# Five score bursts for two head groups in place of six, and mixing two bursts behind, in the attention stage of a hybrid block

## The chip, the cores and the metric

The kernel runs on one core of a Trainium2 chip. The metric is the device time of one execution in microseconds (us); the number given for the kernel before is the median of 8 runs. The engines are named as the profile does: PE is TensorE's matrix multiplication and PEld its weight load, DVE is VectorE, ACT is ScalarE, POOL is GpSimd, SP is SyncE, whose queue issues most of the DMAs.

## What is computed

The input x has 8 batches of 512 rows of 256 numbers, all in fp32. The block is a chain of two mixers, each followed by the same kind of expert layer, each with layer norm ahead and a residual sum behind. The first mixer is a state scan. The second is causal attention with 16 heads of 16 numbers each, and it is the one that matters here:

```
def attn(x, Wqkv, Wout):
    qkv = einsum('btd,ed->bte', x, Wqkv).reshape(b, t, 3, H, DK).transpose(2, 0, 3, 1, 4)
    q, k, v = qkv[0], qkv[1], qkv[2]
    scores = clip(einsum('bhtd,bhsd->bhts', q, k) / sqrt(DK), -10.0, 10.0)
    attn = softmax(scores + triu(full((t, t), -1e9), k=1), axis=-1)
    out = einsum('bhts,bhsd->bhtd', attn, v).transpose(0, 2, 1, 3).reshape(b, t, d)
    return einsum('btd,ed->bte', out, Wout)
```

The expert layer has 16 experts of which each row takes 4 (chosen within 2 of 4 groups), and two shared experts that every row passes through.

## The kernel before

**Stages.** The program has four stages one after another: the scan stretch, the routed experts of the first expert layer, the attention stretch, and the routed experts of the second. `stretch(layer)` writes a mixer batch by batch, and puts beside it, so that TensorE has work: the projections of the next batch (`project`), the shared experts of the batch two before (`shared_experts`), the route of the batch before (`Route`: layer norm, logits, choice of the experts, places, sending of the rows by indirect DMA), and the load, layer norm and turning of the batch two ahead. Loading a batch in the attention stretch means two DMAs (`load_sum`, L152 to L165): the tile `more` and the tile `x`, which VectorE then adds in two halves (L163). The load of `x` stands in SP's queue behind the store of the batch before and behind the store of its normed rows. Only batches 2 to 7 are loaded so, during batches 0 to 5; batches 0 and 1 were readied in the stage before.

**What sets the order.** A mixer is a generator that yields after each portion of matmuls the number of columns that it has streamed. `beside()` (L346) always takes the next portion of the piece that has done the smallest share of its columns; `timed()` (L362) puts the steps of a chain of small operations at given shares of the whole: the two halves of the load's sum at 0.24 and 0.28, the layer norm of the batch ahead from 0.32 to 0.44 and from 0.56 to 0.64, the route's steps at 0.0 to 0.95. A scheduler then sets the instructions on the engines; where they wait follows from the tiles that they share. Each engine works its own queue in order.

**PSUM.** In the attention stretch the pool `one` has four banks, which the projections `pq` (queries and keys) and `pv` (values), the accumulators `po`, the route's `pl` and `pr`, the shared experts' `pg` and `pd` and the output projection `py` take in turn, and the pool `pair` has two tiles of two banks for scores. A bank comes free when its last reader is done: for `pr` that is the addition of `where_m` (L713), for a key projection it is the copy L1196 on VectorE, which makes the second of two key tiles.

**Attention.** The 16 heads of a batch are two halves `o` of 8 heads; a half has two groups `w` of 4 heads (`HG`). The 4 heads of a group lie in four row groups of 32 partitions and are worked by TensorE side by side. Scores are made transposed: for a chunk `c` of 128 keys, all queries from the chunk's first on are columns, so that chunk 0 has 512, chunk 1 has 384, chunk 2 has 256 and chunk 3 has 128. `weights()` (L1223) makes one burst: the scores (L1240) of the chunks named in `BANKS[i]` into two `pair` tiles (two heads each), the exponential of each tile on ScalarE (L1251), and the clamps on VectorE: L1254 for the square on the diagonal, which also masks, and L1262 for the rest. `BANKS` gives a group three bursts: chunk 0 (512 columns), chunks 3 and 1 (128 and 384), chunk 2 (256). The results of full bursts lie in one of 6 "es" spots of the idle expert weights `w_all` (`spot`, L1151), those of the 256-column burst in a work tile `es_a` of the tag "col".

`mix()` (L1267) multiplies the values with the results of a burst (L1275) and sums them up in `po`, a bank for each group; the values have a column of ones, so that the sum of the weights comes along. `share()` (L1285) turns `po` round (L1288), divides, and after the second group turns the half back for the output projection. `steps()` (L1300) puts them in order: with each burst of a group goes the mixing of the burst of the same number of the group before, so mixing lags by three bursts, and a group's mixing ends while the next but one has not begun. In batches 2 to 6 (`close`) scores and mixing are yielded as one portion; in 0, 1 and 7 other work may come between them.

Of the kernel before, what the change touches and what calls it, by code (L numbers as in the profile page):

```python
# [10 lines left out]
FP = mybir.dt.float32  # L11
AF = mybir.ActivationFunctionType
ALU = mybir.AluOpType
AX = mybir.AxisListType

P = 128
SQ = 32
QUAD = P // SQ
B, T, D = 8, 512, 256
# [7 lines left out]
NO = H * DK // P  # L27
# [32 lines left out]
KB, COLS = 9, 6  # L60
# [10 lines left out]
ATT_SCALE = 0.25  # L71

TOP, LOW = float(np.exp(CLIP)), float(np.exp(-CLIP))

BANKS = [((0,), 4 * P), ((3, 1), 4 * P), ((2,), 2 * P)]


@with_exitstack  # L80
def tile_hybrid_block(
# [22 lines left out]
    nc = tc.nc  # L104
# [3 lines left out]
    work = ctx.enter_context(tc.tile_pool(name="work", bufs=2))  # L108
# [4 lines left out]
    def bank(shape, name: str, kind: str = "one"):  # L113
        kind = instead.get(kind, kind)
        return stage[kind].tile(shape, FP, tag=kind, name=name)
# [153 lines left out]
    causal = const.tile([P, 2, P], FP, name="causal")  # L269
# [27 lines left out]
    groups = const.tile([P, P // E], FP, name="groups")  # L297
# [177 lines left out]
    def add_projection(b: int, lhs_of, w_sb, n: int, tag: str):  # L475

        x_sb = x_tiles[b]
        for half in range(2):
            py = bank([P, 2, D], f"py_{tag}_{half}")
            for j in range(2):  # L480
                t = 2 * half + j
                for c in range(n):
                    nc.tensor.matmul(  # L483
                        py[:, j, :],
                        lhsT=lhs_of(c)[:, t * P : (t + 1) * P],
                        rhs=w_sb[:, c, :],
                        start=(c == 0),
                        stop=(c == n - 1),
                    )
                yield n * D  # L490
            rows = x_sb[:, 2 * half : 2 * half + 2, :]
            nc.vector.tensor_add(rows, py, rows)
# [658 lines left out]
    def spot(kind: str, rows: int):  # L1151
        first, many, n = spots[kind]
        spots[kind][2] = (n + 1) % many
        at = first_expert * WEXP + (first + n) * NT * D
        return w_all[:, at : at + NT * D].rearrange("p (a b) -> p a b", a=rows)

    class Attention:
# [60 lines left out]
        def main(self, b: int, made):  # L1218
            q_sb, k_sb, v_sb = made
            tag = f"a{b}"  # L1220
            held = {}

            def weights(o: int, w: int, i: int, at):  # L1223


                tiles, cols = BANKS[i]
                ps, es = [], []
                for two in range(2):
                    name = f"{tag}_{o}_{w}_{i}_{two}"
                    ps.append(bank([P, 2, T], f"ps_{name}", "pair"))  # L1230
                    if cols == T:
                        es.append(spot("es", 2))
                    else:
                        es.append(work.tile([P, 2, cols], FP, tag="col", name=f"es_{name}", bufs=COLS))
                col = 0
                for c in tiles:
                    n = T - c * P
                    for j in range(HG):
                        r = slice(32 * j, 32 * j + 32)
                        nc.tensor.matmul(  # L1240
                            ps[j // 2][:, j % 2, col : col + n],
                            lhsT=k_sb[w][r, o, c * P : (c + 1) * P],
                            rhs=q_sb[r, o, c * P : T],
                            start=True,
                            stop=True,
                        )
                        at[c, j] = es[j // 2][:, j % 2, col : col + n]
                    col += n
                mixed = len(tiles) * P
                for two in range(2):  # L1250
                    nc.scalar.activation(es[two], ps[two][:, :, 0:cols], AF.Exp, scale=ATT_SCALE)  # L1251
                    diagonal = es[two][:, :, 0:mixed]
                    limit = causal[:, 0 : len(tiles), :].rearrange("p c q -> p (c q)")
                    nc.vector.scalar_tensor_tensor(  # L1254
                        diagonal,
                        diagonal,
                        LOW,
                        limit.unsqueeze(1).to_broadcast([P, 2, mixed]),
                        ALU.max,
                        ALU.min,  # L1260
                    )
                    nc.vector.tensor_scalar(es[two][:, :, mixed:], es[two][:, :, mixed:], LOW, TOP, ALU.max, ALU.min)  # L1262
                return T + (len(tiles) - 1) * T

            order = [c for tiles, _ in BANKS for c in tiles]

            def mix(o: int, w: int, i: int, at):  # L1267


                if i == 0:  # L1270
                    at["po"] = bank([P, T], f"po_{tag}_{o}_{w}")
                for c in BANKS[i][0]:
                    for j in range(HG):
                        h = 8 * o + 2 * j + w
                        nc.tensor.matmul(  # L1275
                            at["po"][32 * j : 32 * j + 32, c * P : T],
                            lhsT=v_sb[:, c, h * VC : h * VC + 32],
                            rhs=at[c, j],
                            start=(c == order[0]),
                            stop=(c == order[-1]),  # L1280
                            tile_position=(0, 32 * j),
                        )
                return len(BANKS[i][0]) * T

            def share(o: int, w: int, at):  # L1285

                tr = work.tile([P, T // SQ, SQ], FP, tag="col", name=f"tr_{tag}_{o}_{w}", bufs=COLS)
                nc.vector.transpose(tr.rearrange("p q c -> p (q c)"), at["po"])  # L1288
                rec = small.tile([P, T // SQ], FP, tag="rec", name=f"rec_{tag}_{o}_{w}")
                nc.vector.reciprocal(rec, tr[:, :, DK])  # L1290
                both = held.setdefault(o, tr)
                nc.vector.tensor_mul(
                    both[:, :, w * DK : (w + 1) * DK],
                    tr[:, :, 0:DK],
                    rec.unsqueeze(2).to_broadcast([P, T // SQ, DK]),
                )
                if w == 1:
                    nc.vector.transpose(held["oT"][:, o, :], both.rearrange("p q c -> p (q c)"))

            def steps():  # L1300
                held["oT"] = work.tile([P, NO, T], FP, tag="kb4", name=f"oT_{tag}", bufs=KB)
                groups = [(o, w, {}) for o in range(NO) for w in range(2)]

                close = 1 < b < B - 1
                last = None
                for o, w, at in groups:
                    for i in range(len(BANKS)):


                        columns = weights(o, w, i, at)  # L1310
                        if last is not None and not close:
                            yield columns
                            columns = 0
                        if last is not None:
                            columns += mix(*last[0:2], i, last[2])
                        yield columns
                    if last is not None:
                        share(*last)
                        yield 0
                    last = o, w, at  # L1320
                for i in range(len(BANKS)):
                    yield mix(*last[0:2], i, last[2])
                share(*last)
                yield 0
                yield from add_projection(b, lambda c: held["oT"][:, c, :], wo_sb, KD, tag)

            return Piece(2 * NO * 2 * NT * T + NT * KD * D, steps())


# [48 lines left out]
    def stretch(layer):  # L1378
# [40 lines left out]
        def first_two():  # L1419

            layer.load(1)
            issue(Piece(0, norm(1, True)))
            for _ in range(2):
                pending.pop(0)()
            main = layer.main(0, made.pop(0))
            issue(Piece(0, some(main.steps, NI)))
            issue(Piece(0, turn(1)))
            issue(project(1))
            second = layer.main(1, made.pop(1))
            issue(Piece(0, some(second.steps, NI)))  # L1430
            issue(main)
            return Piece(second.columns - NI * KD * T, second.steps)
# [185 lines left out]
```

## Time and profile before

| what | us |
|---|---|
| median of 8 runs (lowest, highest) | 1718.51 (1715.83, 1723.56) |
| profiled execution: time | 1715.33 |
| profiled execution: span | 1713.6 |
| PE busy in the span | 1603.8 (94%) |
| DVE busy | 1149.7 (67%) |
| ACT busy | 750.2 (44%) |
| attention stage, from the first score to the last output projection | 772.8 to about 1242 |
| scores L1240 in it | 121.7 |
| mixing L1275, full bursts and 256-column ones | 73.3 and 21.1 |

The mean granted clock of TensorE is 0.977 over the span and 1.00 from 765 to 1184 us. The first scores of the batches start at 772.82, about 818, 867, 931.75, 995.37, 1058.77, 1122.91 and 1185.57 us: the middle batches take 63 to 64 us each. The page gives busy times by engine and, for the costliest groups of instructions, line, engine, operation, tiles (out<-in), busy time and the mean in ns, and after the bar the idle time of the engine just before them with what ended it. In a timeline the columns are start, length, engine, line, operation and tiles, how many instructions are gathered in the row, and in brackets the idle time before. TensorE's matmuls overlap, so the cost of one group is best read from its start to the start of the next.

### The profile page before, as it was taken

The numbers are of one execution on the slowest core, as the hardware profiler recorded it, in microseconds if no ns is written. First come the engines' busy times: TensorE is split into PE (matmuls) and PEld (weight loads), VectorE is DVE, ScalarE is ACT, GpSimd is POOL, SyncE is SP. The second block draws the span as 40 slices with busy tenths as digits, with TensorE's granted clock in tenths as the row PEclk, the third lists the DMA queues.
The fourth block names the chain that finished last, engine by engine and source line by source line (L and its number), as shares of the span: only waits on it lengthen the run. The fifth ranks groups of instructions, "written<-read, shape, count | busy, mean of one in ns | idle before, by whom it ended". The sixth has DMA issues, their size and how long they took to land.

```text
span 1713.6 us, 34252 instructions
## 1 busy us (share of the span) xinstructions
PE 1603.8 (94%) x9996; PEld 1162.4 (68%) x9996; DVE 1149.7 (67%) x3685; ACT 750.2 (44%) x1494; POOL 758.8 (44%) x655
## 2 busy tenths in 40 slices
PE   6899995969999999999999999999996999999996
PEld 3566663649999999983344444444355999999995
DVE  7977875525667766646887977967752566666664
ACT  3222322115555555546544444443312555555553
POOL 3355554525555555550022422422451555555554
PEclk8999998989999999999999999999998999999998
DMA  4354422436777766641233323232542767777776
GB/s 162 125 182 167 136 85 81 166 88 98 105 116 122 106 98 97 100 62 37 75 97 120 97 85 120 85 94 76 163 166 68 106 92 129 133 133 135 133 134 132
DMA packets 278815, 192.95 MB, mean 113 GB/s; under 512 B 167041, under 2 KB 260001, under 8 KB 278625
## 3 DMA queue, kind: packets, MB, share of 16 engines
q1 hardware_dynamic: 225536, 117.04, 27.0%
q0 software_dynamic: 51984, 72.09, 23.7%
q8 instruction: 85, 1.39, 0.3%
q10 hardware_dynamic: 1104, 1.57, 0.3%
q14 instruction: 106, 0.86, 0.2%
HBM read 87.36 MB, written 103.23 MB: 111 GB/s over the span
## 4 chain that ended last, share of the span: by engine, by line
PE 35%; DVE 8%; DMA 5%; issue 2%; SPq 2%; ACT 1%; another core or an unknown queue 0%; POOL 0%; POOLq 0%; DVEq 0%; ACTq 0%
PE ph L990 11%; PE pyr L1021 5%; PE ps_a L1240 4%; DMA part<-rows 4%; PE pg_m L1102 3%; PE po_a L1275 3%; PE pd_m L1131 3%; PE pq_a L1185 2%; PE pv_a L1203 1%; PE py_a L483 1%; SPq L944 1%; DVE w_all L1254 1%; DVE act_m L1118 1%; DVE w_all L1262 1%; DVE sig_m L1117 1%
## 5 line engine op out<-in xcount | busy, mean ns | idle before, releaser
L1031 POOL DMA_INDIRECT part<-rows x272 | 426.5, 1568 | 345.9 <-ACT rows L1030 223.4
L756 POOL DMA_INDIRECT xg<-sorted_m,slots_m x256 | 257.7, 1007 | 329.2 <-ACT slots_m L753 75.3
L990 PEld LDWEIGHTS ph<-rows,gate 128*128 128x128 f32 x2160 | 279.0, 192 | 29.7 <-ACT rows L973 17.6
L990 PE MATMUL ph<-rows,gate 128*128 128x128 f32 x2160 | 291.7, 278 | 0.0
L990 PE MATMUL ph<-rows,up 128*128 128x128 f32 x2160 | 285.6, 275 | 0.0
L1021 PE MATMUL pyr<-w_all,rows 128*128 x1088 | 278.9, 380 | 0.0
L990 PEld LDWEIGHTS ph<-rows,up 128*128 128x128 f32 x2160 | 263.3, 192 | 0.0
L963 DVE COPY up<-w_all 128x512 f32 x270 | 119.2, 442 | 213.7 <-PE ph L990 183.6
L963 ACT COPY gate<-w_all 128x512 f32 x270 | 166.3, 618 | 118.9 <-DVE up L963 51.5
L1021 PEld LDWEIGHTS pyr<-w_all,rows 128*128 128x128 f32 x1088 | 187.0, 192 | 14.4
L1030 ACT ACTIVATE rows<-pyr,gain 128x256 f32<-128x256 f32 x272 | 128.7, 473 | 80.6 <-PE pyr L1021 55.3
L998 ACT ACTIVATE rows<-ph 128x256 f32<-128x256 f32 x272 | 104.3, 383 | 120.1 <-PE ph L990 99.6
L1251 ACT ACTIVATE w_all<-ps_a 128x1024 f32<-128x1024 f32 x128 | 124.5, 1020 | 55.7 <-PE ps_a L1240 46.0
L1000 DVE TENSOR_TENSOR rows<-ph,rows 128x256 f32<-128x256 f32 x272 | 115.2, 423 | 43.5 <-ACT rows L998 30.4
L1240 PE MATMUL ps_a<-w_all 32*128 32x384 f32 (+3 forms) x1024 | 121.7, 470 | 11.9 <-ACT w_all L1251 10.2
L1001 DVE TENSOR_TENSOR rows<-ph,rows 128x256 f32<-128x256 f32 x272 | 115.2, 424 | 25.7 <-PE ph L990 0.8
L1102 PE MATMUL pg_m<-xT_m,su_sb 128*128 128x512 f32 x256 | 124.7, 609 | 0.0
L1131 PE MATMUL pd_m<-sd_sb,act_m 128*128 128x256 f32 x512 | 122.2, 383 | 1.7 <-DVE act_m L1118 1.5
L1102 PE MATMUL pg_m<-xT_m,sg_sb 128*128 128x512 f32 x256 | 122.3, 600 | 0.0
L1131 PEld LDWEIGHTS pd_m<-sd_sb,act_m 128*128 128x128 f32 x512 | 95.4, 190 | 26.9 <-issue 7.0
L1240 PEld LDWEIGHTS ps_a<-w_all 32*128 32x128 f32 x1024 | 48.2, 184 | 77.9 <-ACT w_all L1251 30.3
L1102 PEld LDWEIGHTS pg_m<-xT_m,sg_sb 128*128 128x128 f32 x256 | 47.1, 192 | 58.3 <-issue 51.1
(218 smaller groups left out, 2062.2 us busy)
## 6 DMA issues: line engine op xcount, KB each, us to landing
rows<-xg SPq DMA_DIRECT2D x712, 32.0 KB
rows<-xg SPq DMA_DIRECT2D x94, 134.0 KB
part<-x SPq DMA_DIRECT2D x16, 512.0 KB
part<-ys_m SPq DMA_DIRECT2D x14, 512.0 KB
sum<-part SPq DMA_DIRECT2D x14, 512.0 KB
w_all<-in_L_ffn_gate_w_dram SPq DMA_DIRECT2D x24, 256.0 KB
w_all<-in_L_ffn_up_w_dram SPq DMA_DIRECT2D x24, 256.0 KB
w_all<-in_L_ffn_down_w_dram SPq DMA_DIRECT2D x24, 256.0 KB
```

The source lines that it names most:

```text
L756: nc.gpsimd.indirect_dma_start(out=xg[i], out_offset=bass.IndirectOffsetOnAxis(ap=slots[:, at : at + 1], axis=0), in_=rows[:, t, :], in_of ...
L963: copy(here, w_all[:, bass.ds(held[n][0] + half * KD * F, KD * F)])
L990: nc.tensor.matmul(ph[s][:, f * P : (f + 1) * P], lhsT=both[s][:, k * F + f * P : k * F + (f + 1) * P], rhs=rows[:, ROW + k * P : ROW + (k ...
L1000: nc.vector.tensor_mul(act, ph[0], act)
L1001: made = nc.vector.tensor_mul(act, ph[1], act)
L1021: nc.tensor.matmul(py, lhsT=act[:, f * P : (f + 1) * P], rhs=w_all[:, bass.ds(w + 2 * KD * F + f * D, D)], start=(f == 0), stop=(f == KF - 1),
L1030: nc.scalar.mul(y, py, gain[:, TK : TK + 1])
L1031: acc = nc.gpsimd.indirect_dma_start(out=parts[i][n % 2], out_offset=bass.IndirectOffsetOnAxis(ap=rows[:, D + 2 * TK : D + 2 * TK + 1].bit ...
L1102: made = nc.tensor.matmul(dst, lhsT=w[:, k, f * P : (f + 1) * P], rhs=xnT[:, k, :], start=(k == 0), stop=(k == KD - 1),)
L1131: nc.tensor.matmul(py[:, j, :], lhsT=acts[n][:, f, t * P : (t + 1) * P], rhs=shared[n][3][:, f, :], start=(n == 0 and f == 0), stop=(n == ...
L1240: nc.tensor.matmul(ps[j // 2][:, j % 2, col : col + n], lhsT=k_sb[w][r, o, c * P : (c + 1) * P], rhs=q_sb[r, o, c * P : T], start=True, st ...
L1251: nc.scalar.activation(es[two], ps[two][:, :, 0:cols], AF.Exp, scale=ATT_SCALE)
```

## The change

`BANKS` now gives the five bursts of a half, each entry a pair of group and chunk. Both groups' chunks 2, of 256 columns each, share one burst, with their group-0 columns first. All results lie in the "es" spots, so no `es_a` tiles are left. The exponential of every burst covers 1024 columns; for the shared burst the clamps take the two diagonal squares and the two rests together. Mixing lags by `LAG` = 2 bursts, whatever the group; the accumulators of both groups of a half are open at the same time. The rest of `main`, and every other stage, has the same text.

```
-BANKS = [((0,), 4 * P), ((3, 1), 4 * P), ((2,), 2 * P)]
+BANKS = [((0, 0),), ((0, 3), (0, 1)), ((1, 0),), ((0, 2), (1, 2)), ((1, 3), (1, 1))]
+LAG = 2
...
-            def weights(o: int, w: int, i: int, at):
...
+            def weights(o: int, i: int, at):
+
+
+                ps = [bank([P, 2, T], f"ps_{tag}_{o}_{i}_{two}", "pair") for two in range(2)]
+                es = [spot("es", 2) for _ in range(2)]
                 col = 0
-                for c in tiles:
+                for w, c in BANKS[i]:
...
+                    nc.scalar.activation(es[two], ps[two], AF.Exp, scale=ATT_SCALE)
+                    if len({w for w, _ in BANKS[i]}) > 1:
+                        each = es[two].rearrange("p j (w q) -> p (j w) q", w=2)
+                        diagonal, full = each[:, :, 0:P], each[:, :, P:]
+                        limit = causal[:, 0, :].unsqueeze(1).to_broadcast([P, 4, P])
+                    else:
...
+                    nc.vector.scalar_tensor_tensor(diagonal, diagonal, LOW, limit, ALU.max, ALU.min)
+                    nc.vector.tensor_scalar(full, full, LOW, TOP, ALU.max, ALU.min)
...
+            def mix(o: int, i: int, at):
+
+
+                ended = []
+                for w, c in BANKS[i]:
+                    places = [c for which, c in order if which == w]
+                    if c == places[0]:
+                        at["po", w] = bank([P, T], f"po_{tag}_{o}_{w}")
...
+                    if c == places[-1]:
+                        ended.append(w)
+                return len(BANKS[i]) * T, ended
...
-                groups = [(o, w, {}) for o in range(NO) for w in range(2)]
+                made = [{} for _ in range(NO)]
+                bursts = [(o, i, made[o]) for o in range(NO) for i in range(len(BANKS))]
...
-                last = None
-                for o, w, at in groups:
-                    for i in range(len(BANKS)):
...
+                for n in range(len(bursts) + LAG):
+                    columns, ended = 0, []
+                    if n < len(bursts):
+                        columns = weights(*bursts[n])
+                        if n >= LAG and not close:
                             yield columns
                             columns = 0
...
+                    if n >= LAG:
+                        o, i, at = bursts[n - LAG]
+                        more, ended = mix(o, i, at)
+                        columns += more
+                    yield columns
+                    for w in ended:
+                        share(o, w, at)
                         yield 0
```

In the changed kernel's text the lines up to L1223 stand one lower (L164 is L163 of before, L714 is L713, L1197 is L1196, L1204 is L1203); scores are L1234, the exponential L1244, the clamps L1254 and L1255, mixing L1270, and `po` is turned round at L1285.

More of the change, by code (lines that the diff above doesn't have):

```diff
@@ L1221, in main @@
             held = {}
-            def weights(o: int, w: int, i: int, at):
[L1226 to L1234, printed above, removed]
+            def weights(o: int, i: int, at):
+                ps = [bank([P, 2, T], f"ps_{tag}_{o}_{i}_{two}", "pair") for two in range(2)]
+                es = [spot("es", 2) for _ in range(2)]
                 col = 0
-                for c in tiles:
+                for w, c in BANKS[i]:
                     n = T - c * P
@@ L1246, in weights @@
                         )
-                        at[c, j] = es[j // 2][:, j % 2, col : col + n]
+                        at[w, c, j] = es[j // 2][:, j % 2, col : col + n]
                     col += n
-                mixed = len(tiles) * P
                 for two in range(2):
[L1251 to L1272, printed above, removed]
+                    nc.scalar.activation(es[two], ps[two], AF.Exp, scale=ATT_SCALE)
[4 more added lines that the diff above has]
+                    else:
+                        mixed = len(BANKS[i]) * P
+                        diagonal, full = es[two][:, :, 0:mixed], es[two][:, :, mixed:]
+                        limit = causal[:, 0 : len(BANKS[i]), :].rearrange("p c q -> p (c q)")
+                        limit = limit.unsqueeze(1).to_broadcast([P, 2, mixed])
@@ new lines, in weights @@
+                    nc.vector.scalar_tensor_tensor(diagonal, diagonal, LOW, limit, ALU.max, ALU.min)
+                    nc.vector.tensor_scalar(full, full, LOW, TOP, ALU.max, ALU.min)
+                return len(BANKS[i]) * T
+            order = [key for keys in BANKS for key in keys]
+            def mix(o: int, i: int, at):
[4 more added lines that the diff above has]
+                        at["po", w] = bank([P, T], f"po_{tag}_{o}_{w}")
@@ L1275, in mix @@
                         nc.tensor.matmul(
-                            at["po"][32 * j : 32 * j + 32, c * P : T],
+                            at["po", w][32 * j : 32 * j + 32, c * P : T],
                             lhsT=v_sb[:, c, h * VC : h * VC + 32],
-                            rhs=at[c, j],
-                            start=(c == order[0]),
-                            stop=(c == order[-1]),
+                            rhs=at[w, c, j],
+                            start=(c == places[0]),
+                            stop=(c == places[-1]),
                             tile_position=(0, 32 * j),
                         )
-                return len(BANKS[i][0]) * T
+                    if c == places[-1]:
+                        ended.append(w)
+                return len(BANKS[i]) * T, ended
             def share(o: int, w: int, at):
                 tr = work.tile([P, T // SQ, SQ], FP, tag="col", name=f"tr_{tag}_{o}_{w}", bufs=COLS)
-                nc.vector.transpose(tr.rearrange("p q c -> p (q c)"), at["po"])
+                nc.vector.transpose(tr.rearrange("p q c -> p (q c)"), at["po", w])
                 rec = small.tile([P, T // SQ], FP, tag="rec", name=f"rec_{tag}_{o}_{w}")
@@ L1301, in steps @@
                 held["oT"] = work.tile([P, NO, T], FP, tag="kb4", name=f"oT_{tag}", bufs=KB)
-                groups = [(o, w, {}) for o in range(NO) for w in range(2)]
+                made = [{} for _ in range(NO)]
+                bursts = [(o, i, made[o]) for o in range(NO) for i in range(len(BANKS))]
                 close = 1 < b < B - 1
-                last = None
-                for o, w, at in groups:
-                    for i in range(len(BANKS)):
-                        columns = weights(o, w, i, at)
-                        if last is not None and not close:
+                for n in range(len(bursts) + LAG):
[3 more added lines that the diff above has]
+                        if n >= LAG and not close:
                             yield columns
                             columns = 0
[L1314 to L1318, printed above, removed]
-                        yield 0
[L1320 to L1324, printed above, removed]
+                    if n >= LAG:
[5 more added lines that the diff above has]
+                        share(o, w, at)
+                        yield 0
                 yield from add_projection(b, lambda c: held["oT"][:, c, :], wo_sb, KD, tag)
```

## The prediction

> **What bounds the kernel now.** I read the page first, then the table of busy times by stretch, the waits of TensorE inside the attention stage, its timeline in one batch, and the chain of waits. On the page:
>
> ```profile
> PE 1603.8 (94%) x9996; PEld 1162.4 (68%) x9996; DVE 1149.7 (67%) x3685; ACT 750.2 (44%) x1494; POOL 758.8 (44%) x655
> ...
> L1251 ACT ACTIVATE w_all<-ps_a 128x1024 f32<-128x1024 f32 x128 | 124.5, 1020 | 55.7 <-PE ps_a L1240 46.0
> L1240 PE MATMUL ps_a<-w_all 32*128 32x384 f32 (+3 forms) x1024 | 121.7, 470 | 11.9 <-ACT w_all L1251 10.2
> ```
>
> TensorE is the wall; ScalarE mostly waits for scores, and TensorE waits only 10.2 us in all for its exponentials. Where? The table by stretch, one row about a batch (length, then busy time of PE, PEld, DVE, ACT, POOL, and the granted clock):
>
> ```profile
> 800.00:870.00 70.00, 63.70 (x472) 28.58 (x472) 58.03 (x170) 33.23 (x46) 4.53 (x5) 1.00 0.29 79
> ...
> 996.50:1060.00 63.50, 63.08 (x391) 29.29 (x390) 50.50 (x157) 28.14 (x48) 20.14 (x20) 1.00 0.34 102
> ...
> 1184.00:1250.00 66.00, 58.39 (x371) 26.97 (x370) 52.48 (x175) 24.76 (x44) 25.58 (x28) 0.97 0.45 146
> ```
>
> The reader is to see two kinds of batch: in the middle ones (2 to 6) TensorE is busy for 99% and VectorE for 80%; in 0, 1 and 7 TensorE is idle for 6 to 8 us. From 933 to 1124 us TensorE's whole waiting is:
>
> ```profile
> PE pd_m L1131 <- DVE act_m L1118: 1.0, 3, 0.3
> PE pv_a L1203 <- DVE where_m L713: 0.2, 1, 0.2
> ```
>
> The second, 0.2 us long, is the tip of a second chain, as long as TensorE's own work. The chain of waits goes through it in batch 5:
>
> ```profile
> 1064.67 5.62 DMA x<-part
> ...
> 1070.48 0.69 DVE x L163
> ...
> 1075.15 0.14 DVE where_m L713
> ...
> 1075.34 1.13 PE pv_a L1203 x4
> ```
>
> A row load lands, VectorE (held until then at L163, its queue in order) works off what is queued behind, and the last of that frees the bank that the value projection needs. In batches 3, 4, 5 VectorE waited 4.03, 3.81, 4.56 us there. This chain, not its busy share, makes VectorE dangerous.
>
> **What goes.** Only the attention stage (770 to 1242 us) changes; in the others the two programs have the same order. Timeline of TensorE in batch 4:
>
> ```profile
> 1008.45 1.07 PE L1275 MATMUL po_a<-w_all,v_a 128*32 128x128 f32 x16
> ...
> 1012.25 0.70 PE L1240 MATMUL ps_a<-w_all 32*128 32x256 f32 x4
> 1012.88 1.13 PE L1203 MATMUL pv_a<-w_att,xT_l 128*128 128x256 f32 x4
> 1013.94 0.70 PE L1240 MATMUL ps_a<-w_all 32*128 32x256 f32 x4
> ...
> 1028.00 0.71 PE L1240 MATMUL ps_a<-w_all 32*128 32x256 f32 x8
> ...
> 1035.69 1.15 PE L1240 MATMUL ps_a<-w_all 32*128 32x128 f32 x16
> ```
>
> From start to start, a score burst of 512 columns takes 1.07 us (8 matmul passes), one of 128 and 384 takes 1.08 (16 passes), one of 256 takes 0.64: half the columns cost 60%. So about 0.2 us of a burst is fixed, and it is not per matmul. Two bursts of 256 make 1.28; joined, 1.08 by the 16-pass row. Per half 1.07+1.08+0.64 twice is 5.58, after it is 1.07+1.08+1.07+1.08+1.08 = 5.38: 0.4 per batch. More lies in the splits. The burst of 256 at 1012.25 was cut in two by the value projection and cost 0.63 twice, 0.63 lost, and two others started 0.17 and 0.47 later than their columns explain (they follow an exponential closely). I add up the twelve score bursts of batch 4, by starts, to 13.53 us. In the changed program's order there are ten, one still cut (+1.05, as at 1016.20 before) and the first follow-up still late (0.17): 10.76+1.22 = 11.98. **Saved on scores 1.55.** Mixing bursts go 1.00, 1.00, 0.57: 10.39 by starts in batch 4, after it ten of 1.00: **saved 0.39.** Together 1.94 per middle batch.
>
> The Trainium skill, "TensorEngine Tiling (Array Packing)", section Instruction Overhead, says that each matmul carries about 60 cycles. The change keeps the number of score matmuls, so by that rule the burst merging saves nothing, and dropping 1.94 in eight batches would put my sum at about 15 us slower. The equal 1.07 and 1.08 of 8 and 16 passes speak for a cost per burst, so I go by the rows.
>
> ScalarE: 8 x 1.02 + 4 x 0.60 = 10.56 per half become 10 x 1.02 = 10.2. VectorE: the clamps of a half lose 1.1/2 us. Both run beside TensorE, which is busy for 63.1 of 63.5 us: nothing counted. If that cover were gone, as in batches 0, 1 and 7, at most 0.36 and 0.55 us per half would count, and they lie within the bounds taken there. No DMA is added or taken away; in SP's queue one store changes places with one load in batch 1, and I cost it at nothing (the load at L163 there was 1.96 us late, which bounds it).
>
> **What comes.** Mixing now follows its scores by two bursts instead of three, and both accumulators of a half overlap, so one bank of the four single ones is held longer. The mix of two bursts ago is ready after exp 1.02 and clamps 0.60+0.34; between lie a whole burst and its exponentials (2 x 1.02), so it waits only where VectorE's queue is late.
>
> There it is late, in the batches that load rows (2 to 5). Let S be the start of L163; in batch 4 S = 1006.34 = 10.97 after the batch's first score (995.37). Before: L163 0.61, one clamp pair 0.94, statistics 0.34, the key copy L1196 0.66, aggregate 0.09, two clamp pairs of the 256 tiles 0.51 each, statistics and four row sums 0.33+0.09+0.09+0.11+0.30, where_m 0.2: S+4.8 = 15.8, and TensorE reaches the value projection at 15.9. Just in time. In the changed order, ahead of the same instruction stand also the second L163 (0.61), three more statistics with aggregates (1.1), and bigger clamps (0.80 in place of 0.51, twice): S+7.26 = 18.2. And TensorE, with the shorter bursts, has only 15.0 us of work up to it. It waits in three places: the fourth key projection for the copy L1196 (its bank), the second half of a mix for the clamp behind L163, and the value projection for where_m; in sum until 18.35, **3.3 us**. The second value projection's bank is that of the fourth key projection, whose copy now stands behind the route's chain: **0.9 to 1.0.** So 4.3 of stall against 1.94 saved: +2.4 for each of batches 3, 4, 5. Batch 2 waits for no load at L163 (its 2.46 us of idle there ended with an issue): I take +0.6, from bounds of -1.9 and +2.4. Batch 6 loads nothing: -1.9.
>
> Batches 0, 1, 7 are not packed (`close` is false); there the score bursts wait for the two score tiles. Waits for L1251 are 10.2 us in the stage, 3.8 of them after 1184. Two bursts fewer per batch and no split ones: walked through the new order I get -2.2 (bounds -4 and 0) for batch 0, -2.4 (same bounds) for 1, where two mixes wait for clamps behind the route's VectorE work. Batch 7, not walked in full: -1.5, from -3.8 (all waits gone) to +1.0 (the route's own 1.04 wait at 1232 doubled).
>
> Sum: 3 x 2.4 + 0.6 - 1.9 - 2.2 - 2.4 - 1.5 = -0.2 us, on 1715.33 of the profiled execution (span 1713.6). That execution is 3.2 under the median of the runs, 1718.51; on that scale I predict 1718.3.
>
> **Rivals.**
> *Faster: the row load does not bind.* If TensorE isn't stalled (rows land 4 us earlier against the batch's start, or the scheduled statistics are cheaper behind one another), batches 2 to 6 give -1.94 each, the others -6.1: -15.8, 1702.7. Half the stalls left: -7, 1711. For it: VectorE has 13 us of idle in a middle batch, 4 of them in this very wait, so the chain alone carries the stall. Against it: a queue in order can't use that idle time.
> *Slower: two bursts are too short a lag where the route's VectorE chain stands between scores and mix.* Batches 0, 1, 7 have VectorE busy for 80% with chains of 3 to 5 us of small instructions. Each clamp that falls behind such a chain delays a mix, and with it the bank and the score tiles. From the point where this costs the 6.1 us gained there, the loading batches' +5.9 stands alone: 7.2+0.6-1.9 = +5.9, 1724.4. For it: with a lag of three the mixes of before already waited 0.7 us in two places for a clamp (L1262).
> *The joining doesn't do what it says:* if the joined burst is broken up by other work in most batches, or its 16 passes cost what two bursts do, only about 0.66 of 1.94 is saved: 8 x 1.28 = +10, 1728.5. The new order keeps it whole in batch 4; a small chance.
>
> **How the numbers follow.** Less than 0.2% (3.4 us) is about what a measurement of this kernel can tell from no change. Stalls and savings cancel: 0.37, between 1715 and 1722. Not binding: 0.34. Lag too short: 0.24. Not joined: 0.05. With every bound at its low end together the sum would be -21.5, at its high end +8.7; neither is likely whole. The range goes from 1705, most of the first rival, to 1728, the second and nearly the third. Faster 0.34, same 0.37, slower 0.29.
>
> **What would show it.** Step by step: ten score bursts a batch instead of twelve, the joined one 1.07 to 1.08 us from start to start; TensorE waits of 3 us before L1204 (on where_m) and before the key projection in batches 3, 4, 5, nothing of it in 6; first scores of batches 3 to 5 about 65.8 apart instead of 63.5, batch 6 about 60.8; fewer waits on the exponential in 0, 1, 7. I am wrong if the loading batches shrink too, if clamps hold the mixes up in batches 0, 1, 7, or if a joined burst takes 1.28.

## The result, and the profile after

The changed kernel took 1724.52 us in the median of 14 runs (1720.35 to 1730.31), the kernel before 1718.74 in 39: a ratio of 1.0031, 95% interval 1.0021 to 1.0042. It is 0.3% slower. Predicted were 1718.3 us, between 1705 and 1728; the likeliest case was no change (0.37), slower had 0.29. The profiled execution took 1725.55 us (span 1723.8, mean granted clock 0.972), 10.2 more than that of before, which lay 3.4 below its median (1715.33). The two profiles so show a larger difference than the medians do; by batches they show where it lies:

| batch | before | after | difference | predicted |
|---|---|---|---|---|
| 0 | 45.86 | 43.22 | -2.6 | -2.2 |
| 1 | 48.78 | 49.72 | +0.9 | -2.4 |
| 2 | 64.29 | 66.23 | +1.9 | +0.6 |
| 3 | 63.62 | 68.21 | +4.6 | +2.4 |
| 4 | 63.40 | 67.93 | +4.5 | +2.4 |
| 5 | 64.14 | 68.82 | +4.7 | +2.4 |
| 6 | 62.66 | 60.79 | -1.9 | -1.9 |
| 7 | 57.34 | 56.17 | -1.2 | -1.5 |
| sum | 470.1 | 481.1 | +11.0 | -0.2 |

(From a batch's first score to the next batch's, the last to the end of its output projection, in us; the predicted column is worked out in the prediction.) The page of the changed kernel, busy times and the group of the scores:

```profile
PE 1597.2 (93%) x9996; PEld 1166.1 (68%) x9996; DVE 1151.9 (67%) x3621; ACT 747.0 (43%) x1462; POOL 761.4 (44%) x655
...
L1234 PE MATMUL ps_a<-w_all 32*128 32x128 f32 (+3 forms) x1024 | 113.8, 481 | 8.8 <-ACT w_all L1244 8.0
```

TensorE is busy for 6.6 us less than before (1603.8), and the span is 10 longer: the time went into waits and, as the account of the prediction shows further down, into a slower clock. The five largest waits of TensorE from 765 to 1260 us, the columns being total, number and longest:

```profile
PE pv_a L1204 <- DVE where_m L714: 9.7, 4, 2.5
PE po_a L1270 <- DVE w_all L1254: 8.2, 7, 2.3
PE ps_a L1234 <- ACT w_all L1244: 8.0, 14, 1.8
PE pg_m L1103 <- DVE act_m L1119: 5.9, 6, 1.2
PE pq_a L1186 <- DVE w_all L1197: 1.7, 4, 0.4
```

Four of these five are on VectorE: `where_m`, a clamp (L1254), the gates (the shared experts' matmuls `pg` wait for a bank that `act_m`, L1119, reads last) and the key copy (L1197). In the kernel before, the wait on where_m came to 0.2, that on a clamp (L1262) to 0.7, and those on the gates and the key copy to less than 0.2. What holds VectorE is seen in its timeline in batch 4, whose first score starts at 999.31:

```profile
1011.52 0.69 DVE L164 TENSOR_TENSOR x<-x,more 128x512 f32<-128x512 f32 x1 [5.05 <-DMA x<-part]
1012.14 0.68 DVE L1254 SCALAR_TENSOR_TENSOR w_all<-w_all,causal 128x512 f32<-128x512 f32 x1
1012.74 0.42 DVE L1255 TENSOR_SCALAR w_all<-w_all 128x512 f32<-128x512 f32 x1
1013.07 0.68 DVE L164 TENSOR_TENSOR x<-x,more 128x512 f32<-128x512 f32 x1
1013.67 0.74 DVE L1197 TENSOR_SCALAR w_all<-pq_a,parity 128x512 f32<-128x512 f32 x1
...
1017.86 0.79 DVE L711 TENSOR_TENSOR row_m<-pr_m,row_m 128x16 f32<-128x16 f32 x4
1018.57 0.21 DVE L714 TENSOR_TENSOR where_m<-pr_m,row_m 128x64 f32<-128x64 f32 x1
```

and what waits for it in TensorE's:

```profile
1009.97 1.15 PE L1234 MATMUL ps_a<-w_all 32*128 32x256 f32 x16
1011.04 0.41 PE L1270 MATMUL po_a<-w_all,v_a 128*32 128x128 f32 x4
1012.88 1.18 PE L1270 MATMUL po_a<-w_all,v_a 128*32 128x128 f32 x12 [1.42 <-DVE w_all L1254]
1014.47 1.98 PE L1186 MATMUL pq_a<-xT_l,w_att 128*128 128x512 f32 x4 [0.42 <-DVE w_all L1197]
1018.93 1.65 PE L1204 MATMUL pv_a<-w_att,xT_l 128*128 128x256 f32 x4 [2.48 <-DVE where_m L714]
1020.51 2.09 PE L1234 MATMUL ps_a<-w_all 32*128 32x128 f32 x16
1022.53 1.15 PE L1270 MATMUL po_a<-w_all,v_a 128*32 128x512 f32 x8
...
1052.57 1.98 PE L1103 MATMUL pg_m<-xT_m,su_sb 128*128 128x512 f32 x4 [1.24 <-DVE act_m L1119]
```

VectorE sits for 5.05 us before the load's sum, then everything that TensorE asks for comes out one behind the other: the clamp at 1012.14, the key copy at 1013.67, where_m at 1018.57. The joined burst itself costs what was said: 1.07 us from 1009.97 to 1011.04. The burst behind the longest wait, of 128 and 384 columns, takes 2.02 us (1020.51 to 1022.53) where such a burst took 1.08 before; the row of the granted clock further down tells why.

### The profile page after: what moved, and what is told of

The parts are those of the page before. It is cut to its first block, busy times and chain, and to the rows that moved or that the text cites. A ratio compares the mean times of both kernels' runs of the same rounds, so it can differ in the third digit from the quotient of the medians.

```text
span 1723.8 us, 34166 instructions
## 1 busy us (share of the span) xinstructions
PE 1597.2 (93%) x9996; PEld 1166.1 (68%) x9996; DVE 1151.9 (67%) x3621; ACT 747.0 (43%) x1462; POOL 761.4 (44%) x655
## 5 line engine op out<-in xcount | busy, mean ns | idle before, releaser
L757 POOL DMA_INDIRECT xg<-sorted_m,slots_m x256 | 262.1, 1024 | 289.7 <-ACT slots_m L754 94.6
L1244 ACT ACTIVATE w_all<-ps_a 128x1024 f32<-128x1024 f32 x160 | 155.3, 1021 | 91.9 <-PE ps_a L1234 74.8
L1031 ACT ACTIVATE rows<-pyr,gain 128x256 f32<-128x256 f32 x272 | 128.6, 473 | 80.8 <-PE pyr L1022 55.3
L1234 PE MATMUL ps_a<-w_all 32*128 32x128 f32 (+3 forms) x1024 | 113.8, 481 | 8.8 <-ACT w_all L1244 8.0
L1254 DVE SCALAR_TENSOR_TENSOR w_all<-w_all,causal 128x512 f32<-128x512 f32 (+1 forms) x160 | 92.3, 577 | 40.4 <-ACT w_all L1244 39.1
L1270 PE MATMUL po_a<-w_all,v_a 128*32 128x384 f32 (+3 forms) x1024 | 93.4, 452 | 9.2 <-DVE w_all L1254 8.2
```

What stands on the lines that cost most here:

```text
L757: nc.gpsimd.indirect_dma_start(out=xg[i], out_offset=bass.IndirectOffsetOnAxis(ap=slots[:, at : at + 1], axis=0), in_=rows[:, t, :], in_of ...
L1031: nc.scalar.mul(y, py, gain[:, TK : TK + 1])
L1234: nc.tensor.matmul(ps[j // 2][:, j % 2, col : col + n], lhsT=k_sb[w][r, o, c * P : (c + 1) * P], rhs=q_sb[r, o, c * P : T], start=True, st ...
L1244: nc.scalar.activation(es[two], ps[two], AF.Exp, scale=ATT_SCALE)
L1254: nc.vector.scalar_tensor_tensor(diagonal, diagonal, LOW, limit, ALU.max, ALU.min)
```

## The experiments

Each was timed in five rounds against the kernel before on the same chip. The chips differ (before took 1716.0, 1712.7 and 1673.6 us on the three that were used), so the ratios are compared, and the batches of the profiles.

**The load's sum later.** The rows' sum and the norm behind it go behind where_m in VectorE's queue.

```
-                    pieces.append(timed(added, 0.24, 0.28))
+                    pieces.append(timed(added, 0.36, 0.40))
-                    timed(norm(nxt), *spread(0.32, 0.44, NT), *spread(0.56, 0.64, NT)),
+                    timed(norm(nxt), *spread(0.42, 0.50, NT), *spread(0.56, 0.64, NT)),
```

> The changed kernel with the two halves of the load's sum put at 0.36 and 0.40 of the batch instead of 0.24 and 0.28, and the first half of the layer norm behind it at 0.42 to 0.50 instead of 0.32 to 0.44, so that in VectorE's queue they stand behind where_m and the clamps of the first half's bursts. Theory (VectorE stands in its queue before the load and everything that TensorE needs is behind it): in batches 2 to 5 the waits on where_m (9.7 us), on the clamp L1254 (5.9 of 8.2) and on L1197 (2.4) go, some 18 us; about 1706 us. Rival (a lag of two bursts is too short by itself): the waits on the clamps stay and the time stays within 1718 to 1725. Rival (the joined burst brings nothing): batches 2 to 5 do not fall below the 63.5 us of before, the time stays at 1717 or over.

Measured: 1717.17 us, ratio 1.0002 (0.9986 to 1.0017); batches 3 to 5 at 65.4, 66.7 and 65.5. The waits on where_m, clamps and L1197 are gone, all of them, but the gain is not 18 us. TensorE's waits from 765 to 1260:

```profile
PE ps_a L1234 <- ACT w_all L1244: 11.8, 15, 3.3
PE pg_m L1103 <- issue: 7.5, 2, 3.8
PE pg_m L1103 <- DVE act_m L1119: 4.8, 3, 3.8
PE pg_m L1103 <- DVE which_m L683: 3.8, 1, 3.8
```

A new wait of 3.8 us a batch, of the shared experts (`pg`) for a bank. The theory named the right waits and missed that the next one is ready behind them: in batch 4 VectorE is busy with hardly a break from the sum (1020.89 and 1024.23) through the route's choice of experts to the act_m (1043.57) that frees the bank, and, as I read it, both accumulators of the half hold banks. About the end of each of these waits the granted clock falls to 0.50 for 3.4 us, in batch 4 for 6.8.

**A fourth x tile.** A load can then be issued a batch earlier; the room is taken from the col tiles. The order keeps the sum ahead of where_m.

```
-KB, COLS = 9, 6
+KB, COLS = 9, 4
-    xpool = ctx.enter_context(tc.tile_pool(name="xpool", bufs=3))
+    xpool = ctx.enter_context(tc.tile_pool(name="xpool", bufs=4))
```

> The changed kernel with four x tiles instead of three, so that a load need not wait for the batch before to be stored and normed, and with four instead of six col tiles, to make room. VectorE's order keeps the load's sum ahead of where_m. Theory: the rows have landed when VectorE comes to the sum, its wait of 5 us in batches 3 to 5 goes, and with it the waits of TensorE on where_m and the clamps, as in the run with the late sum; 1704 to 1712 us, less what fewer col tiles cost in other stages (unknown, 0 to 10). If it is the order of VectorE's work and not the load that costs, the waits on where_m stay at 2 us or more a batch, and batches 3 to 5 stay at 67 us or more.

Measured: 1702.65 us, ratio 0.9922 (0.9898 to 0.9947), a little under the range of the theory. Batches 1 to 6 take 46.28, 62.80, 62.12, 62.12, 62.12 and 60.77. Its waits from 765 to 1260:

```profile
PE ps_a L1234 <- ACT w_all L1244: 7.0, 12, 1.6
PE pg_m L1103 <- DVE act_m L1119: 6.0, 6, 1.3
PE pv_a L1204 <- DVE w_all L1197: 2.7, 4, 0.8
...
PE pv_a L1204 <- DVE where_m L714: 0.3, 1, 0.3
```

9.7 us on where_m have become 0.3, though the same instructions stand ahead of it. It is the load that VectorE stood before, and the work between is harmless once it is done in time. What stays in each of batches 2 to 5 are two waits for banks: 1.2 on the gates and 0.7 on the key copy.

**The same four col tiles with three x tiles**, as a control:

```
-KB, COLS = 9, 6
+KB, COLS = 9, 4
```

> The changed kernel with four col tiles and three x tiles: the other control. Theory: the fewer col tiles bring nothing; 1722 to 1727 us, VectorE waits for the load and batches 3 to 5 at 68 us as in the changed kernel. Rival: it is the fewer col tiles, and not the load, that made the run with the fourth x tile fast; 1703 to 1710.

Measured: 1723.16, ratio 1.0057 (1.0037 to 1.0076), batches 3 to 5 at 68.0, 67.9, 67.9, and 9.7 us on where_m as in the changed kernel. The fewer col tiles give nothing; the gain is the load's.

**Only the second half of the sum later.** The wait for the load stays, 1.3 to 2 us of work ahead of where_m goes.

```
-                    pieces.append(timed(added, 0.24, 0.28))
+                    pieces.append(timed(added, 0.24, 0.40))
-                    timed(norm(nxt), *spread(0.32, 0.44, NT), *spread(0.56, 0.64, NT)),
+                    timed(norm(nxt), *spread(0.42, 0.50, NT), *spread(0.56, 0.64, NT)),
```

> The changed kernel with only the second half of the load's sum put later (0.40 instead of 0.28) and the first half of the layer norm behind it (0.42 to 0.50); the first half of the sum stays at 0.24, so VectorE still waits for the load. Only the second sum and two of the statistics are no longer ahead of L1197 and where_m, some 1.3 to 2 us of VectorE's queue. Theory (the stall is the load's landing plus what stands between it and where_m): the wait on where_m falls from 2.5 us to 0.5 to 1.2 a batch, that on L1197 ahead of the fourth key projection goes (0.4), that on the clamp behind the load (1.4 to 1.6) stays; batches 3 to 5 at 66 to 66.6 us instead of 68.2, the whole 5 to 7 us faster than the changed kernel. Rival (the load's landing alone sets it): no more than 0.5 us a batch. Rival (the work ahead is all of it): batches 3 to 5 at 64 us or less.

Measured: ratio 1.0029 (1.0013 to 1.0045), no gain; batches 3 to 5 at 67.6, 68.7, 68.5. The waits from 740 to 1270 us say why:

```profile
PE pg_m L1103 <- DVE act_m L1119: 11.1, 6, 2.6
...
PE po_a L1270 <- DVE w_all L1254: 7.6, 6, 2.1
PE pv_a L1204 <- DVE where_m L714: 3.4, 3, 1.1
PE pv_a L1204 <- DVE w_all L1197: 2.9, 4, 0.8
```

The wait on where_m fell to 1.1 as expected and the clamp's stayed; but the gates' wait doubled, from 1.2 to 2.5 a batch. With the key copy's 0.7 (L1197) a batch, what was taken off one bank came back at others, so the batches hardly got shorter, and the expectation of 66 was wrong. The granted clock is halved for 3.4 us in each of batches 3 to 5 here too.

**The late sum in the kernel before**, the same two edits there:

> The kernel before with the same late places for the load's sum and the norm. Theory: TensorE waited 0.2 us in all on where_m in batches 3 to 5 of it, so there is nothing to gain from the load there: within 2 us of before (1717 to 1721), batches 3 to 5 at 63 to 64 us. Rival (the late sum is a gain for any order, by other means): 1 per cent faster, as in the changed kernel.

Measured: 1719.98, ratio 1.0024 (1.0010 to 1.0037); batches 3 to 5 at 64.2, 64.9, 64.2. The rival that a late sum helps any order falls; it costs the order of before 0.2%.

**The lag of two with six bursts**, that is one part of the change without the joining (the results of the 256-column bursts stay in "es" spots, so the run does not part the lag from that):

```
-BANKS = [((0, 0),), ((0, 3), (0, 1)), ((1, 0),), ((0, 2), (1, 2)), ((1, 3), (1, 1))]
+BANKS = [((0, 0),), ((0, 3), (0, 1)), ((0, 2),), ((1, 0),), ((1, 3), (1, 1)), ((1, 2),)]
...
-                    nc.scalar.activation(es[two], ps[two], AF.Exp, scale=ATT_SCALE)
+                    nc.scalar.activation(es[two], ps[two][:, :, 0:col], AF.Exp, scale=ATT_SCALE)
```

(with `es` cut to `col` columns ahead of it)

> The changed kernel with the six bursts of before (256-column ones apart, their results in the es spots) and a lag of two bursts: the lag alone, without the joining. Theory: the second half of the load's sum stays behind where_m in VectorE's order and TensorE has as much work as before up to the value projection, so batches 3 to 5 wait 1 to 3 us, mostly on the clamp behind the load; 1718 to 1723 us. Rival (the short lag makes the loss): 1724 us or more, with the same waits as in the changed kernel, batches 3 to 5 at 68 us or more.

Measured: 1709.33 us, ratio 0.9956 (0.9938 to 0.9974): faster than before, against the expectation and against the rival, though the waits of 1 to 3 us a batch came as expected. Batches 2 to 6 take 60.47, 64.28, 64.49, 65.34 and 59.88. Two lines of TensorE in batch 6 show the difference to the order of before, where each such burst at this place was cut in two by the value projection:

```profile
1138.44 2.98 PE L1204 MATMUL pv_a<-w_att,xT_l 128*128 128x256 f32 x12
1141.35 0.71 PE L1234 MATMUL ps_a<-w_all 32*128 32x256 f32 x8
1141.99 1.07 PE L1271 MATMUL po_a<-w_all,v_a 128*32 128x512 f32 x8
```

By starts, the scores of batch 6 take 13.54 us before, 12.02 joined, 11.41 with six whole bursts. With one accumulator open at a time there is no wait on a bank in that batch at all, against 0.81 us on the gates when joined. Of the waits in the loading batches one is left:

```profile
PE ps_a L1234 <- ACT w_all L1245: 11.2, 20, 2.2
PE po_a L1271 <- DVE w_all L1255: 6.5, 3, 2.9
```

a mix waiting for the clamp that stands behind the load, 1.7, 1.9 and 2.9 us in batches 3 to 5. About the end of each of them the granted clock falls to 0.50 for 3.4 us; in batch 2, without such a wait, it stays at 1.00.

**The same with the fourth x tile** (the two edits of that run on top):

> Six bursts with a lag of two, and the fourth x tile (four col tiles). In the run of six bursts with a lag of two, batch 6, which loads nothing, took 59.9 us and batches 3 to 5 64.3 to 65.3, with 6.5 us of waits on a clamp behind the load. Theory (the load in VectorE's queue is all that holds them up): batches 2 to 5 come to about 60 us, 14 us less than without the fourth tile: about 1695 us, and the joined bursts with the same tile (batches 3 to 5 at 62.1) lose 2 us a batch to it. Rival (the joining has a worth of its own that only the load hides): no faster than 1702.65, the joined bursts with the fourth tile.

Measured: 1700.85, ratio 0.9930 (0.9910 to 0.9950). Batches 2 to 5 come to 60.5 each, as expected, 1.6 to 2.3 us less than the joined bursts. The time is not 1695, since batches 0 and 1 took 49.2 and 50.1, where the joined bursts took 44.6 and 46.3. In those the joining has a worth of its own, so neither theory holds for the whole.

**The kernel before with the fourth x tile**, as the control for both:

> The kernel before with the fourth x tile and four col tiles: the control of both runs with that tile. Theory: TensorE hardly waits for the load there, so 1713 to 1720 us, batches 3 to 5 at 62.7 to 63.5 us as batch 6. Rival (an earlier load is worth 20 us to any order): 1703 or less, as with the joined bursts.

Measured: 1737.99, ratio 1.0135 (1.0112 to 1.0158), slower. Its longest wait in sum from 765 to 1270:

```profile
PE pd_m L1131 <- DVE tr_a L1288: 7.6, 5, 1.8
```

The output of the shared experts waits for a bank until `po` is turned round into a col tile. The results of the 256-column bursts lie in col tiles too in this order, and four are fewer than it was made for; I take that for the cause, but no run tells it. So the control may be spoilt by the room that it needed, and what an earlier load alone gives to the order of before stays open.

**The changed order in batches 0, 6 and 7 alone**, that of before in 1 to 5 (`main` of before is kept beside the new one):

```
+JOINED = (0, 6, 7)
...
+            if b not in JOINED:
+                return self.main_six(b, made)
```

> The changed order in batches 0, 6 and 7 alone, the order of before in 1 to 5. Theory (the change gains 2.6, 1.9 and 1.2 us in these three, by the batches of the two profiles, and loses in 1 to 5 by clamps and loads): 5.7 us faster than before, 1711 to 1714. Rival (what the change gains at one place is lost at the next, since the end of the stage is set elsewhere): within 2 us of before.

Measured: 1706.99, ratio 0.9967 (0.9952 to 0.9982), 5.7 us less than before. By batches of its profile 0, 6 and 7 gained 4.0, 1.9 and 0.8, and 1 to 5 lost 1.5 together. The gains in these three batches are real; so the loss of the changed kernel lies in 1 to 5.

**The best of each**: joined bursts in batches 0 and 1, six with a lag of two in 2 to 7, four x tiles.

```
+APART = [((0, 0),), ((0, 3), (0, 1)), ((0, 2),), ((1, 0),), ((1, 3), (1, 1)), ((1, 2),)]
+JOINED = (0, 1)
...
+            bank_list = BANKS if b in JOINED else APART
```

> The best of what the runs showed in one kernel: the fourth x tile and four col tiles, joined bursts in batches 0 and 1 (44.6 and 46.3 us with that tile), six bursts with a lag of two in batches 2 to 7 (60.5 four times, 59.9, 56.7). Theory: the batches add up, 91 + 418 us from the first score to the last output projection = 449 against 458 with six bursts throughout: 8 us less than the six bursts with the fourth tile, ratio to before about 0.988. Rival (in batches 0 and 1 the two differ by the execution and not by the order): the same ratio as six bursts with the fourth tile, 0.993.

(The addition in that text should read 91 + 358.) Measured: ratio 0.9867 (0.9849 to 0.9884), 1652.94 against 1673.59 us on its chip; batches 44.4, 46.3, 60.6, 60.5, 60.7, 60.5, 59.9, 55.3, in sum 448.2 where 449 was expected. It is 1.3% faster than before and the best version found.

## Why the prediction was wrong

**What held.** The fixed 0.2 us of a burst, not of a matmul: the joined burst of 16 passes took 1.07. The chain that was to eat the savings is the one that did: load, VectorE's queue, key copy, clamp, where_m. From L164 to the end of where_m it took 7.26 us in batch 4, as predicted (the parts listed there add up to 7.07). Batch 6, which has no load, fell by the 1.9 us of the forecast, but in part by luck: TensorE's time apart from waits fell by 2.7, and 0.8 came back as a wait on the gates that was not foreseen. Batches 0 and 7 came within 0.4, while batch 0 alone ranged from 41.83 to 44.28 us among the profiles of this order with three x tiles.

**The step that failed is the size of the stall in the loading batches.** It was put at 4.3 us in each of batches 3 to 5, against 1.94 saved, for a loss of 2.4; the loss was 4.6, 4.5 and 4.7. In the trace TensorE's idle time there rose by 5.4, 5.2 and 5.8 us, and the rest of its time fell by only 0.9, 0.7 and 1.1. Three terms were too low or missing, and one did not come.

- **The start of the chain.** S was carried over from before as 10.97 us after the batch's first score, the lowest of three (11.2, 11.0 and 11.7 in batches 3 to 5). It was 12.4, 12.2 (1011.52 - 999.31) and 13.1 in the changed kernel, and the waits up to the value projection came to 4.5, 4.3 and 5.2 us instead of 3.3. In batch 4 the load was issued as late as before (5.9 us after the first score) and took 6.18 us to land, not 4.94. The trace has sixteen completions of this load: fifteen came within 4.82 us (before 4.86), so one straggler made it late. Every lag-of-two order with three x tiles and the sum at 0.24 shows a late start (12.2 in batch 4 with six bursts, with four col tiles and with the second half late), but the order of before has it at times too: 12.0, 11.1 and 11.8 in the mixed kernel. The load shares the DMA engines with the turning of the rows (`through_m` and `share_m`); why one part lands later is not settled.
- **The gates.** The wait of the shared experts on their gates, 1.2 us a batch, wasn't in the walk. I followed the four banks only up to the second value projection, though I had written that one bank is held longer; with both accumulators open it is missing for `pg` too. That the six bursts, with one accumulator open, show no such wait in batch 6, and that the runs with a late sum move the wait to just this place, speaks for it; no run took the bank pressure away by itself, so it is argued more than shown.
- **The clock.** The walk took TensorE's pace from the kernel before, whose granted clock is 1.00 all through these batches. In the changed kernel it is halved for 3.4 us in each of batches 3, 4 and 5, from 951.1, 1019.3 and 1087.6 us on, within 0.5 us of the end of the wait on where_m. The stretch in batch 4 and the one after it, in the columns of the prediction's table (the granted clock is third from the end):

```profile
1019.30:1022.80 3.50, 3.50 (x24) 1.62 (x26) 3.36 (x11) 0.67 (x3) 0.90 (x1) 0.51 0.00 0
1022.80:1087.60 64.80, 58.50 (x368) 28.09 (x360) 47.19 (x135) 27.14 (x41) 19.96 (x20) 1.00 0.33 100
```

With the fourth x tile the wait is gone, the clock stays at 1.00 from batch 2 to 5, and TensorE's time apart from waits is 60.2 us in each of batches 3 to 5, against 62.3 to 62.4 here. So a slower pace cost 2.1 to 2.2 us a batch; the halved clock can explain at most 1.7 of it (half of 3.4, an estimate). In batch 2, where the clock was not halved, the same comparison gives 0.6. What halves it is not settled: a wait of 2.26 us on where_m in batch 2 did not, and one of 2.26 us at the same place with four col tiles did.
- **The term that did not come.** The wait for the copy of the fourth key projection, put at 0.9 to 1.0, is not in the trace of batches 3 to 5. It came in batch 2 (0.74 us) and with the fourth x tile (0.7), where TensorE gets there at the full clock.

The saving itself was put too low. With the fourth x tile scores and mixing take 12.02 and 9.95 us in batch 4, as worked out, but TensorE's time apart from waits falls by 2.8 against before and not by 1.94: the rest lies in groups that the sum left alone.

**Batch 2** was given +0.6 because its idle time at L163 carried no DMA's name; it lost 1.9, with 2.3 us on where_m like the others. An unnamed wait ahead of a load's sum should have been taken for the load: in the kernel before its last part landed at 878.78, and L163 began at 878.85. **Batch 1** was given -2.4 and lost 0.9. VectorE waited there for the load too, 3.44 us (before 1.96), and mixes waited 3.2 us for clamps. With the load out of the way (fourth x tile) the same order took 46.28 in batch 1, 2.5 less than before: the walk was right except for the load.

**The rivals.** The first, that the load does not bind, was priced at 1702.7; with the fourth tile it came to 0.9922 of before, 1705 on the scale of the 1718.5. Its mechanism was right and its price near, its condition wasn't met. The second, that a lag of two is too short, falls as a cost of the lag itself: with six bursts it is faster than before by 0.4%, though a mix does wait for its clamp in batches 3 to 5, where VectorE stands before a load. The third falls with the joined burst of 1.07 us. I had ascribed the saving to the joining and the danger to the lag. In the packed batches the joining saves TensorE nothing over six bursts with the same lag: with the fourth tile its time apart from waits in batch 4 is 60.2 us in both. Six bursts spend less on scores (11.41 against 12.02 in batch 6, since none is cut up) and more on mixing and other groups. What differs are the waits, 1.9 us with the joined bursts and 0.2 with six.

## What to carry to other kernels

An engine that works its queue in order and meets a load in the middle of it is as late as that load for everything behind it; its mean busy share says nothing of this. When a bound engine is made faster, look for a second chain that is just in time (here a wait of 0.2 us), carry over not only its length but the spread of its start, check whether the bound engine keeps its clock behind a longer wait, and follow every shared buffer to the end of the stage: a stall taken away at one bank reappeared at the next, until the load itself was moved ahead. Test the parts of a change apart: in the packed batches the part that was thought to carry the gain cost it, and the other one brought it.

## What the runs showed of the hardware

A load of 512 KB took 4.5 to 7.1 us from issue to landing at the same point of batches 3 to 5 in the orders with three x tiles, the late ones by a single straggler of sixteen parts (in batch 4 of the changed kernel 4.82 us for fifteen, 6.18 for the last). Bursts of score matmuls on four row groups carry about 0.2 us each, whether of 8 or 16 passes (512 columns 1.07 and 1.08 us, 256 columns 0.64), and where another stream cuts a burst in two, either part takes as long as the whole: 0.63 us each for a 256-column burst that takes 0.64, and 1.05 and 1.06 for a 512-column one that takes 1.07. The granted clock of TensorE fell to 0.50 for 3.4 us or twice that about the end of waits of 1.7 to 3.8 us in batches 2 to 5, but not at every such wait (2.26 us in batch 2 of the changed kernel). The kernel before took 1673.6 us on one chip and 1712.7 to 1718.7 on others. Between 200 and 400 us, where the two programs have the same text, the granted clock was 0.91 in the profile of before and 0.98 in that of the best version, which ran on the fast chip; no run tells the chip's share in this.
